# Moving two sets of quarter sums from GpSimd to VectorE in a two-layer attention kernel

## The chip, the core and the metric

The kernel runs on one core of one Trainium2 chip. The metric is the time of one execution on the device, in microseconds (us). Five engines with a queue each take part: TensorE (PE in the profile; its weight loads are PEld), VectorE (DVE), ScalarE (ACT), GpSimd (POOL) and SyncE (SP), which issues most DMAs.

## The reference, cut to what matters

Two attention blocks follow each other on `x`, 8 samples of 512 channels and 32 x 32 = 1024 positions, all in float32. The change lies in the second block, layer 1, which has one head of 512 channels:

```python
n = (x - mean) * jax.lax.rsqrt(var + EPS)          # mean and var over a whole sample
q = jnp.einsum('oc,bcs->bos', wq, nf) + bq[None, :, None]
k = jnp.einsum('oc,bcs->bos', wk, nf) + bk[None, :, None]
v = jnp.einsum('oc,bcs->bos', wv, nf) + bv[None, :, None]
attn = jnp.einsum('bci,bcj->bij', q, k) * c ** (-0.5)
attn = jax.nn.softmax(attn, axis=-1)
out = jnp.einsum('bcj,bij->bci', v, attn)
out = jnp.einsum('oc,bcs->bos', wo, out) + bo[None, :, None]
return x + out.reshape(b, c, h, w)
```

## The kernel before, in words

**Products in fewer multiplications.** Large products are made by Strassen's method in Winograd's form: both operands are cut into quarters, sums of quarters (S1 to S4 on one side, T1 to T4 on the other) are formed, and seven products of quarters replace eight. Many products use it twice: each of the seven operands is itself cut into quarters and gets its own four sums. `halve_a(name)` (L1594) makes those four second-level sums for one operand of the scores; it calls `sums_a` (L506), whose instruction is L520: four `tensor_tensor` of 128 x 256 from SBUF to SBUF, into a new buffer of the pool `t` (36 buffers of 128 x 1024, L89). The second depends on the first and the fourth on the second. A helper records them, so all have line L520; in the profile the output is `S_twice` or `A_twice` where the buffer is of pool `t`, and `spare` where it is of the weights' pool.

**Order.** PE, ACT and DVE run their instructions in the order of the program text (`manual_schedule`, L2215). `at_steps(steps, hooks)` (L765) runs a generator and, behind its n-th step, the functions listed under n: that is how side work is placed between products. `together` (L753) takes steps of two generators by turns. POOL and SP get their order from the framework's planner; POOL takes up an instruction as soon as its inputs and its buffer are free, however early that is against the other engines.

**Layer 1 of one sample**, in the order in which it runs (all samples but the last, which takes another branch and is not touched by the change):

1. A form of q is made (`make_q_twice`, L1700) in quarters `z_q` and `c_q`.
2. V is made by `make_v_twice` (L1057) through `by_two_steps` (L627): 14 steps of pairs of second-level products (steps 0 to 13, tiles `ps_s_v` and `ps_o_v`), then *V's lines*, six steps of 8 matmuls (14 to 19, tile `ps_l_v`, L793). In the pairs VectorE evicts at L644; in the lines it evicts at L665 and adds c22 onto c12 at L670 ahead of each of steps 14 and 15. Hooks here: `finish_q(1..4)` (L1780, instruction L1787, tile `s_q`) behind steps 5, 7, 9 and 11 makes the first-level sums of q, each two 128 x 512 additions on VectorE; `halve_a` of A11 behind step 3 and of S2 and S1 behind step 18, on POOL.
3. *Phase one* of the scores: `twice` (L1832) for A11*B11 and S2*T2 by turns, 14 steps of 4 matmuls (L1841, tiles `ps_l` and `ps_s`). Inside one `twice` the products go by turns into two PSUM banks, `line` (products 1, 3, 5, 7) and `single` (2, 4, 6). ScalarE copies products 1, 3, 4 and 7 to the tiles `p` (L1855), VectorE adds products 2, 5 and 6 to them (L1851). Hooks: POOL's `halve_a` of S4 and A22 (step 0), VectorE's of A12 (1) and S3 (4), and T3's sums (6).
4. *The S1 stage*: `twice` for S1*T1 alone, 7 steps. Since no other `twice` is interleaved, each product comes back to a bank two products later, and has to wait until that bank is evicted. Hooks: `onto_second(k)` (L1907) adds one 128 x 1024 tile of `p` to another on VectorE, SBUF to SBUF (L1908); `onto_third(k)` (L1910) copies its result on ScalarE; `with_p5` (L1891, instruction L1894) is another 128 x 1024 addition on VectorE.
5. *The A12/S3 phase* and *the S4/A22 phase*, 14 steps each, then the softmax's sums and the product with V.

GpSimd meanwhile runs, in this order: A11's sums, S2's, S1's, a few tiny statistics of a later sample (L350 to L356), S4's and A22's, then `sum_v` (L1966, instruction L1973, tile `s_v`): four additions of 128 x 512 of V's quarters into two buffers of pool `t`, and A12's second-level sums of V.

Of the kernel before, what the change touches and what calls it, by code (L numbers as in the profile page):

```python
# [65 lines left out]
def two_attention_blocks(  # L66
# [18 lines left out]
    nc = tc.nc  # L85
# [16 lines left out]
    def tile2(name):  # L102
        return tpool.tile([P, 2, HALF], FP, tag="t", name=name)
# [402 lines left out]
    def sums_a(q, t, engine=nc.vector, made=range(1, 5)):  # L506

        t = t if len(t.shape) == 2 else flat(t)
        n = t.shape[1] // 4
        for i in range(4):  # L510
            part = t[:, i * n : (i + 1) * n]
            if len(q["A11"].shape) == 3:
                part = part.rearrange("p (u o) -> p u o", u=2)
            q[f"S{i + 1}"] = part
        for i, x, y, op in [
            (1, "A21", "A22", ALU.add), (2, "S1", "A11", ALU.subtract),
            (3, "A11", "A21", ALU.subtract), (4, "A12", "S2", ALU.subtract),
        ]:
            if i in made:
                engine.tensor_tensor(q[f"S{i}"], q[x], q[y], op)  # L520
        return q
# [227 lines left out]
    def in_turn(*groups):  # L749
        for g in groups:  # L750
            yield from g

    def together(*groups):  # L753

        groups = list(groups)
        spares.clear()
        while groups:
            for g in list(groups):
                if next(g, g) is g:
                    groups.remove(g)  # L760
                else:
                    yield
        spares.clear()

    def at_steps(steps, hooks):  # L765

        n = -1
        for n, _ in enumerate(steps):
            for hook in hooks.get(n, []):
                hook()  # L770
        assert n >= max(hooks, default=-1)
# [209 lines left out]
    def flat(t):  # L981
        return t.rearrange("p h n -> p (h n)")
# [74 lines left out]
    def make_v_twice(w, twice_a, bs, twice_b, pairs, name):  # L1057


        parts = twice_a.all(columns_of(w))  # L1060

        def multiply(bank, n, x, y, start):
            for i, (a, v) in enumerate(PAIRS[n]):
                for u in range(2):
                    nc.tensor.matmul(  # L1065
                        bank[:, (2 * i + u) * P : (2 * i + u + 1) * P],
                        twice_b[v][y][:, u * P : (u + 1) * P], parts[a][x],
                        start=start and i == u == 0, stop=True, skip_group_check=True,
                    )

        def multiply_line(i, bank, a, v, start):
            by_positions(w.parts[0], i, bs)(bank, a, v, start)

        def at(n, r, t):
            both = flat(pairs[n][t]).rearrange("p (m o) -> p m o", m=4)
            return both[:, :, r * P : (r + 1) * P]

        return by_two_steps(multiply, multiply_line, pairs, at, None, name)
# [496 lines left out]
    def attention1(xs, norm, ready, b, at_values, norms):  # L1575
# [18 lines left out]
        def halve_a(name, t=None, engine=nc.vector):  # L1594
            q = {
                f"A{i + 1}{j + 1}": of[name][j][:, i * 2 * P : (i + 1) * 2 * P]
                for i in range(2) for j in range(2)
            }
            twice_a[name] = sums_a(q, flat(tile2(f"{name}_twice_{b}")) if t is None else t, engine)
# [131 lines left out]
        of, hooks_v, biases = {}, {}, []  # L1731
# [60 lines left out]
        if last:  # L1792
            hooks_v[17] = [lambda: halve_a("S1")]
        else:
            for n, name in [(3, "A11"), (18, "S2"), (18, "S1")]:
                hooks_v.setdefault(n, []).append(lambda name=name: halve_a(name, None, nc.gpsimd))
        at_steps(make_v_twice(w, twice_w[0], bs, twice_b, v_pairs, f"v_1_{b}"), hooks_v)


# [17 lines left out]
        def line(t):  # L1817


            bank = banks("s", f"ps_s_1_{b}_{t}")[:, 0, :]  # L1820
            c11, c12, c21 = (ps[j][t // 2][i] for i, j in [(0, 0), (0, 1), (1, 0)])
            for a, v, places in [("A11", "B11", [c11]), ("S2", "T2", [c12, c21])]:
                for k in range(2):
                    nc.tensor.matmul(  # L1824
                        bank, bs[v][:, k, t * P : (t + 1) * P], of[a][k],
                        start=a == "A11" and k == 0, stop=k == 1, skip_group_check=True,
                    )
                for to in places:
                    nc.scalar.copy(to[:, t % 2, :], bank)
                yield  # L1830
# [60 lines left out]
        def with_p5(i, j, k):  # L1891

            to, other = ps[j][k][i], ps[1][k][1] if i == 0 else ps[0][k][1]
            nc.vector.tensor_tensor(to, to, other, ALU.add)  # L1894
# [12 lines left out]
        def onto_second(k):  # L1907
            nc.vector.tensor_tensor(ps[1][k][0], ps[1][k][0], ps[0][k][0], ALU.add)  # L1908

        def onto_third(k):  # L1910
            nc.scalar.copy(ps[0][k][1], ps[1][k][0])

        if last:
            at_steps(
                together(
                    in_turn(together(line(0), line(1)), together(line(2), line(3))),
                    twice("S1", "T1", "oo", 1, 1, True, False),
                ),
                {
                    2: [lambda: halve_a("A12", spare[0])], 5: [lambda: halve_a("S3", spare[1])],  # L1920
                    8: [halve_t3], 14: [lambda: with_p5(0, 1, 0)],
                },
            )
        else:
            at_steps(
                together(
                    twice("A11", "B11", "ss", 0, 0, True, False), twice("S2", "T2", "oo", 0, 1, True, False)
                ),
                {
                    0: [lambda: halve_a("S4", None, nc.gpsimd), lambda: halve_a("A22", None, nc.gpsimd)],  # L1930
                    1: [lambda: halve_a("A12", spare[0])], 4: [lambda: halve_a("S3", spare[1])],
                    6: [halve_t3],
                },
            )
            at_steps(
                twice("S1", "T1", "so", 1, 1, True, False),
                {
                    1: [lambda: onto_second(1)], 3: [lambda: onto_second(0)], 4: [lambda: onto_third(1)],
                    6: [lambda: onto_third(0), lambda: with_p5(0, 1, 1)],
                },  # L1940
            )
# [273 lines left out]
    with tc.manual_schedule(engines={PE, ACT, DVE}):  # L2215
# [76 lines left out]
        for b in range(B):  # L2292
            xs, norm, ready, to = layer0(bs, qs, ks, vs, b, norms.get(b + 1), ending, begun)
            at_values, vs, begun = {}, [], []
            if to is not None:
                qs, ks = to["qs"], to["ks"]
                at_values = {
                    2: [lambda: vs.extend(to["v"].back())],
                    6: [lambda: put_qk(to["qk02"].back(), 0, qs, ks)],
                    10: [lambda: put_qk(to["qk13"].back(), 1, qs, ks)],  # L2300
                    14: [lambda: begun.append(first_score(qs, ks, b + 1))],
                }
            ending = attention1(xs, norm, ready, b, at_values, norms)
# [413 lines left out]
```

## Time and profile before

| what | value |
|---|---|
| time before, median of 3 runs | 2783.01 us (2782.43 to 2783.02) |
| the profiled execution's own time | 2783.47 us |
| span of its instructions | 2781.6 us |
| PE busy | 2763.5 us, 99% of the span |
| DVE busy | 2195.9 us, 79% |
| ACT busy | 1191.2 us, 43% |
| POOL busy | 685.8 us, 25% |
| granted TensorE clock | 0.999 |

The span runs from the first to the last instruction; 1.9 us of the execution's time lie around it. "Busy" is the union of the times of an engine's instructions. Matmuls overlap in the pipeline, so the time that PE loses is best read from the distance between the starts of matmuls: the 128 x 256 matmuls of V's lines and of the scores start 0.216 us apart when nothing holds them, which makes 0.86 us for a product of 4. In the timeline view each row has start, duration, engine, line, operation, out<-in and shape, and in brackets the idle time before it with the instruction that ended it; an instruction that waits inside for a resource shows as a longer duration, not as idle time.

The seven samples that the change touches follow each other 340.8 us apart, and their layer-1 stages agree within some hundredths of a us, the seventh (the one shown here, from 2386 to 2449 us) within a tenth.

### The profile page before, as it was taken

The numbers are of one execution on the slowest core, as the hardware profiler recorded it, in microseconds if no ns is written. First come the engines' busy times: TensorE is split into PE (matmuls) and PEld (weight loads), VectorE is DVE, ScalarE is ACT, GpSimd is POOL, SyncE is SP. The second block draws the span as 40 slices with busy tenths as digits, with TensorE's granted clock in tenths as the row PEclk, the third lists the DMA queues.
The fourth block names the chain that finished last, engine by engine and source line by source line (L and its number), as shares of the span: only waits on it lengthen the run. The fifth ranks groups of instructions, "written<-read, shape, count | busy, mean of one in ns | idle before, by whom it ended". The sixth has DMA issues, their size and how long they took to land. (4 is left out here: it accounts for less than half of the span.)

```text
span 2781.6 us, 42257 instructions
## 1 busy us (share of the span) xinstructions
PE 2763.5 (99%) x16486; PEld 1677.1 (60%) x16486; DVE 2195.9 (79%) x3051; ACT 1191.2 (43%) x1897; POOL 685.8 (25%) x696
## 2 busy tenths in 40 slices
PE   9999999999999999999999999999999999999999
PEld 5437774377743786447864478635686356853375
DVE  6797787877878778887788777887778877888877
ACT  3462533625346153462525524265342643226621
POOL 0001550016400263003630045300552005420121
PEclk9999999999999999999999999999999999999999
DMA  7545514264142642326432263322633236141101
GB/s 257 199 138 197 201 57 141 58 212 182 57 141 58 212 182 80 121 62 231 156 120 82 77 230 141 137 72 75 238 129 140 69 105 238 68 171 31 35 16 40
DMA packets 114528, 358.63 MB, mean 129 GB/s; under 512 B 25052, under 2 KB 25852, under 8 KB 107920
## 3 DMA queue, kind: packets, MB, share of 16 engines
q1 hardware_dynamic: 89856, 299.68, 31.5%
q10 hardware_dynamic: 24464, 56.16, 6.1%
q8 instruction: 132, 2.16, 0.3%
q14 instruction: 76, 0.62, 0.1%
HBM read 252.77 MB, written 79.21 MB: 119 GB/s over the span
## 5 line engine op out<-in xcount | busy, mean ns | idle before, releaser
L950 ACT ACTIVATE p<-s 128x1024 f32<-128x1024 f32 x505 | 516.4, 1024 | 308.4 <-PE s L1146 301.7
L952 DVE TENSOR_TENSOR acc<-acc,p 128x1024 f32<-128x1024 f32 x384 | 468.9, 1221 | 63.3 <-ACT p L950 54.3
L1146 PE MATMUL s<-qk_back,qk_back 64*64 64x512 f32 x3528 | 457.4, 590 | 0.0
L1195 PE MATMUL ps_o<-p,v_back 64*64 64x512 f32 x3528 | 455.3, 589 | 0.0
L537 POOL TENSOR_TENSOR B_twice_p<-o 128x512 f32<-128x512 f32 x14 | 20.9, 1495 | 1065.8 <-DVE o L1215 1065.8
L1195 PEld LDWEIGHTS ps_o<-p,v_back 64*64 64x64 f32 x3528 | 134.9, 133 | 243.6 <-issue 239.8
L1146 PEld LDWEIGHTS s<-qk_back,qk_back 64*64 64x64 f32 x3528 | 132.6, 133 | 245.6 <-issue 216.2
L2035 PE MATMUL ps_o<-t_p,s_v 128*128 128x512 f32 x384 | 169.6, 596 | 0.0
L1815 ACT ACTIVATE p<-p,factor 128x512 f32<-128x512 f32 (+1 forms) x112 | 85.3, 781 | 109.3 <-DVE p L1851 82.7
L537 POOL TENSOR_TENSOR B_twice<-x 128x512 f32<-128x512 f32 x23 | 38.4, 1668 | 358.6 <-DVE x L1457 177.2
L2035 PEld LDWEIGHTS ps_o<-t_p,s_v 128*128 128x128 f32 x384 | 71.8, 190 | 88.4 <-issue 88.0
L665 DVE TENSOR_TENSOR c_v<-ps_l_v,c_v 128x512 f32<-128x512 f32 x120 | 79.9, 687 | 55.1 <-PE ps_l_v L793 55.0
L1851 DVE TENSOR_TENSOR p<-ps_s,p 128x512 f32<-128x512 f32 x140 | 94.0, 685 | 30.2 <-PE ps_s L1841 28.5
L1851 DVE TENSOR_TENSOR p<-ps_l,p 128x512 f32<-128x512 f32 x150 | 101.0, 687 | 21.0 <-PE ps_l L1841 19.3
L952 DVE TENSOR_TENSOR acc<-p,p 128x1024 f32<-128x1024 f32 x57 | 69.7, 1222 | 47.8 <-ACT p L950 47.8
L1855 ACT COPY p<-ps_l 128x512 f32<-128x512 f32 x66 | 38.7, 586 | 146.9 <-PE ps_l L1841 146.9
L1044 PE MATMUL ps_l_qk<-t,w_qk 128*128 128x512 f32 x224 | 98.7, 593 | 0.1
L647 ACT COPY c_q<-ps_s_qk 128x512 f32<-128x512 f32 x56 | 32.6, 583 | 140.8 <-PE ps_s_qk L1037 140.8
L647 ACT COPY c_v<-ps_s_v 128x512 f32<-128x512 f32 x90 | 52.7, 585 | 82.3 <-PE ps_s_v L1065 80.8
L1812 POOL TENSOR_TENSOR acc<-acc,p 128x512 f32<-128x512 f32 x48 | 83.5, 1740 | 13.3 <-ACT p L1815 10.8
L373 POOL TENSOR_TENSOR rstd<-rstd,minus_half 128x4 f32<-128x4 f32 (+1 forms) x16 | 12.9, 806 | 274.2 <-DVE rstd L372 274.2
L1044 PEld LDWEIGHTS ps_l_qk<-t,w_qk 128*128 128x128 f32 x224 | 42.5, 190 | 54.0 <-issue 53.1
(709 smaller groups left out, 5965.8 us busy)
## 6 DMA issues: line engine op xcount, KB each, us to landing
x<-in_x SPq DMA_DIRECT2D x64, 512.0 KB, 8.6
qk_back<-kept_qk SPq DMA_DIRECT2D x56, 512.0 KB, 6.8
w_qk<-stored_qk SPq DMA_DIRECT2D x14, 1792.0 KB
fold<-acc SPq DMA_DIRECT2D x56, 256.0 KB, 3.0
qk_twice<-stored_qk_twice ACTq DMA_DIRECT2D x28, 512.0 KB, 4.8
kept_v<-c_v SPq DMA_DIRECT2D x28, 512.0 KB, 4.3
kept_qk<-c_q SPq DMA_DIRECT2D x28, 512.0 KB, 2.6
kept_qk<-c_k SPq DMA_DIRECT2D x28, 512.0 KB, 3.5
```

The lines of the kernel that those rows point to most:

```text
L537: engine.tensor_tensor(t[:, 0:4:2, :], part[:, :, 2 * P :], part[:, 0, :].rearrange("p (n q) -> p n q", n=2), ALU.subtract,)
L647: nc.scalar.copy(to, of(bank, to))
L665: nc.vector.tensor_tensor(c, bank, c, ALU.add)
L950: nc.scalar.activation(p, s, AF.Exp, scale=factor)
L952: nc.vector.tensor_tensor(acc, first, p, ALU.add)
L1044: nc.tensor.matmul(bank, of(i, a)[:, k, :], bs[v][:, k, :], start=start and k == 0, stop=k == 1, skip_group_check=True,)
L1146: nc.tensor.matmul(s[cols, j, :], ks[pair][k0 // HALF][rows, k0 % HALF : k0 % HALF + HD], qs[pair][g][rows, :], start=True, stop=True,)
L1195: nc.tensor.matmul(o[cols, half, :], vs[n][kt % 4 // 2][rows, h, c0 : c0 + HD], p[rows, j, :], start=kt == 0, stop=kt == NT - 1,)
L1812: engine.tensor_tensor(acc[:, i, :], acc[:, i, :], seen[i][-1], ALU.add)
L1815: nc.scalar.activation(p, p, AF.Exp, scale=norm.factor)
L1851: nc.vector.tensor_tensor(at(r, t), bank, at(r, t), ALU.add)
L2035: nc.tensor.matmul(bank, v_parts[kt // 2][a][:, kt % 2, c * P : (c + 1) * P], p_parts[kt // 2][b][:, kt % 2, cols], start=fresh and kt == ...
```

## The change

It has three parts, all in `attention1` and all for the first seven samples:

- S2's four sums go from POOL to VectorE, at the same place of the text (behind step 18 of V).
- S1's four sums go from POOL to VectorE and behind step 13, the last, of phase one.
- In the S1 stage `onto_second(0)` goes from behind the fourth product to behind the fifth's eviction, and `onto_third(1)` from behind the fifth to behind the fourth. ScalarE has no instruction between these two places, so its own order stays.

```diff
         if last:
             hooks_v[17] = [lambda: halve_a("S1")]
         else:
-            for n, name in [(3, "A11"), (18, "S2"), (18, "S1")]:
-                hooks_v.setdefault(n, []).append(lambda name=name: halve_a(name, None, nc.gpsimd))
+            hooks_v.setdefault(3, []).append(lambda: halve_a("A11", None, nc.gpsimd))
+            hooks_v[18] = [lambda: halve_a("S2")]
         at_steps(make_v_twice(w, twice_w[0], bs, twice_b, v_pairs, f"v_1_{b}"), hooks_v)
...
-                    6: [halve_t3],
+                    6: [halve_t3], 13: [lambda: halve_a("S1")],
                 },
             )
             at_steps(
                 twice("S1", "T1", "so", 1, 1, True, False),
                 {
-                    1: [lambda: onto_second(1)], 3: [lambda: onto_second(0)], 4: [lambda: onto_third(1)],
+                    1: [lambda: onto_second(1)], 3: [lambda: onto_third(1)], 4: [lambda: onto_second(0)],
                     6: [lambda: onto_third(0), lambda: with_p5(0, 1, 1)],
                 },
             )
```

## The prediction

> **What bounds the kernel now.** I read the page first, then TensorE's waits, then the timeline of each engine over one of the seven samples (the one from 2386 us), then the same stretch of the last sample.
>
> ```profile
> span 2781.6 us, 42257 instructions
> PE 2763.5 (99%) x16486; PEld 1677.1 (60%) x16486; DVE 2195.9 (79%) x3051; ACT 1191.2 (43%) x1897; POOL 685.8 (25%) x696
> ```
>
> TensorE is the bound: work taken from another engine counts only where TensorE waits for it.
>
> ```profile
> PE ps_l L1841 <- DVE p L1851: 8.0, 7, 1.2
> PE ps_l_v L793 <- DVE c_v L665: 2.6, 7, 0.4
> ```
>
> TensorE waits for VectorE at two places, seven times each: once a sample. The first is in the S1 stage (TensorE, VectorE, POOL in turn):
>
> ```profile
> 2421.22 1.05 PE L1841 MATMUL ps_s<-S_twice,t 128*128 128x256 f32 x4
> 2423.47 1.13 PE L1841 MATMUL ps_l<-s_q,T_twice 128*128 128x256 f32 x4 [1.20 <-DVE p L1851]
> ...
> 2415.01 0.69 DVE L1851 TENSOR_TENSOR p<-ps_s,p 128x512 f32<-128x512 f32 x1 [0.17 <-PE ps_s L1841]
> 2418.52 0.69 DVE L1851 TENSOR_TENSOR p<-ps_s,p 128x512 f32<-128x512 f32 x1 [2.82 <-PE ps_s L1841]
> 2419.13 3.69 DVE L1908 TENSOR_TENSOR p<-p,p 128x1024 f32<-128x1024 f32 x2
> 2422.74 0.68 DVE L1851 TENSOR_TENSOR p<-ps_l,p 128x512 f32<-128x512 f32 x1
> ...
> 2415.11 2.50 POOL L1973 TENSOR_TENSOR s_v<-c_v,c_v 128x512 f32<-128x512 f32 x2 [11.74 <-PE ps_s L1841]
> 2417.56 2.51 POOL L1973 TENSOR_TENSOR s_v<-s_v,c_v 128x512 f32<-128x512 f32 x2
> ```
>
> The seventh product (2423.47) needs the fifth's bank, whose add (2422.74) stands behind both `onto_second`. See also that VectorE idles 2.82 us ahead of 2418.52, where S1's sums are to go, and that POOL's `sum_v` starts in that hole: it waits for the same product as VectorE's add of 2415.01.
>
> The second place is V's lines: the add of 2396.71, which frees the bank, stands behind slow SBUF additions.
>
> ```profile
> 2393.82 1.84 DVE L1787 TENSOR_TENSOR s_q<-c_q,s_q 128x512 f32<-128x512 f32 x2
> 2395.57 1.21 DVE L670 TENSOR_TENSOR c_v<-c_v,c_v 128x512 f32<-128x512 f32 x1
> 2396.71 0.68 DVE L665 TENSOR_TENSOR c_v<-ps_l_v,c_v 128x512 f32<-128x512 f32 x1
> 2397.31 0.68 DVE L670 TENSOR_TENSOR c_v<-c_v,c_v 128x512 f32<-128x512 f32 x1
> ```
>
> The first L670 takes 1.21 us, the next 0.68: POOL runs S2's and S1's sums from 2389.60 to 2399.22, in turn with VectorE.
>
> **What the skill says.** "SBUF — State Buffer", section "Who interferes with whom": a VectorE instruction with two SBUF inputs contends with a GpSimd one that reads SBUF, and the first to issue has the shared port for its whole length. The trace agrees, and the last sample, where VectorE makes four 128 x 256 sums (into `spare`) beside `sum_v`, has the price:
>
> ```profile
> 2684.74 1.37 DVE L520 TENSOR_TENSOR spare<-spare,q 128x256 f32<-128x256 f32 x1
> 2686.04 1.48 DVE L520 TENSOR_TENSOR spare<-q 128x256 f32<-128x256 f32 x1
> 2687.45 1.49 DVE L520 TENSOR_TENSOR spare<-q,spare 128x256 f32<-128x256 f32 x1
> 2688.86 0.68 DVE L1851 TENSOR_TENSOR p<-ps_s,p 128x512 f32<-128x512 f32 x1
> ...
> 2683.12 2.71 POOL L1973 TENSOR_TENSOR s_v<-c_v,c_v 128x512 f32<-128x512 f32 x2 [3.18 <-issue]
> 2685.80 2.85 POOL L1973 TENSOR_TENSOR s_v<-s_v,c_v 128x512 f32<-128x512 f32 x2
> ```
>
> A sum of 0.42 us alone takes 1.48, one after each POOL addition. Adds that read PSUM (0.69 throughout) don't pay. "VectorE: DVE Perf Modes", section "The TRN2 errata", gives (N+151)/0.96 ns for a float32 addition: 424 ns at 256 columns; measured 411 to 427 without POOL.
>
> **The change part by part**, for one of seven samples. An uncontended set of four sums takes 1.46 us of VectorE (2680.25 to 2681.71 in the last sample, the same four instructions). No DMA is issued or moved; SP's queue stays. On POOL eight additions go, its other work keeps its order.
>
> *POOL loses S2's and S1's sums: -0.97.* Two losses of TensorE lie behind them. V's lines take 11.10 us (2393.35 to 2404.45) in the seven samples, but 10.36 for the same 48 matmuls in the last, where POOL is idle: 0.74. And their first matmul starts 0.37 us behind the last one before it (0.33 in the other samples; 0.11 unheld): some 0.23, since VectorE's add of `ps_o_v` (2392.62, after two `s_q` of 1.05 each) frees that bank late. Uncontended, the four last `s_q` need 4 x 0.60 instead of 2.03 + 1.75, 1.4 us less, and L670 0.5 less: more than either loss. S4's and A22's sums, next on POOL, can't start before `finish_q(4)` has ended (S4 comes first in the queue), so they meet L670 at most. Bounds: 0 (POOL fills the gap with A22 first) to -0.97; I take the whole.
>
> *S2's sums on VectorE in V's lines: +0.10.* They stand between line 0's and line 1's last adds. The first pair starts at 2402.93 and takes 1.20, the sums end at 2405.59, line 1's pair (today 2404.65) then frees its bank at 2406.87 instead of 2405.94. Phase one's fourth product starts at 2407.04 and its weight load, which takes the wait, at 2406.83: late by some 0.09. Behind them on VectorE, A12's sums and the add for product step 2 come 0.95 later; that bank is wanted at 2409.4 and is free at 2408.9. S3's and T3's sums follow without a gap until 2412.5, just when the next add falls due (2412.49): the delay is gone. Bounds 0 to +0.3.
>
> *S1's sums behind phase one, with `sum_v`: +0.93 together with the third part.* Were POOL still, they would fit the hole: 2415.62 + 1.46 = 2417.08, and product 3 wants the second sum at 2418.3. But `sum_v` waits for the buffer it writes, which the product that ends at 2415.0 releases (wait of 11.74 us; seven waits in all, 73.4 us). The change takes as many `t` buffers ahead of `sum_v` as before, so I expect it to get the same one at the same moment, 0.5 us ahead of S1's first sum. Then it goes as in the last sample: from `sum_v`'s start to the add behind the sums 2688.86 - 2683.12 = 5.74, so the add of product 2 starts at 2415.11 + 5.74 = 2420.85 instead of 2418.52. TensorE's queue stands behind it: product 4 needs that bank, 2420.85 + 0.68 + 0.05 = 2421.58 instead of 2419.27. Product 5 follows after 0.97 (as 2423.47 to 2424.44, a product behind a stall), 2422.55; product 6, held by ScalarE's copy of product 4, some 0.9 later, 2423.46.
>
> *`onto_second(0)` behind the fifth's add.* Alone it would be worth -1.31: the fifth's add would run when its product is done, and product 7 start 0.94 behind product 6, 2422.16 instead of 2423.47. After the delay above: fifth product 2422.55, its add 1.12 later (as 2417.40 to 2418.52), 2423.67, so product 7 at 2424.40; the next phase starts at 2425.37 instead of 2424.44: +0.93. The first `onto_second` ends by 2423.2 even with a POOL addition ahead, in time. The second then runs 2424.5 to 2425.7, the sixth's add and `with_p5` to 2427.4, and the first add of the A12/S3 phase at 2427.4 frees its bank by 2428.1; TensorE wants it at 2425.37 + 4 x 0.86 - 0.2 = 2428.6. Covered by 0.5; if not, 0 to +0.4.
>
> Sum: -0.97 + 0.10 + 0.93 = +0.06 a sample, times 7 = **+0.4 us**. On the profiled execution's 2783.47 that is 2783.9; that execution lies 0.46 above the median, so against 2783.01 I say **2783.4**.
>
> **The rivals.**
>
> *Few sums meet `sum_v` (faster).* For it: VectorE has a hole of 2.82 us, and POOL's start hangs on one buffer. Against: the shared wait. Without collision -0.97 + 0.10 - 1.31 = -2.18, times 7 = -15.3: 2767.7. Were `sum_v` one product (0.86) earlier, the add of product 2 comes 0.86 earlier, the stage costs +0.07, and the whole is -0.80 x 7 = -5.6: 2777.4. Chance 0.18.
>
> *POOL's turns stay in V's lines (slower).* A22's inputs are ready before `s_q`'s last sums; if POOL takes A22's four sums into the gap, each still takes its turn with an `s_q`, and V's lines keep their loss. Price +0.97 x 7 = 6.8: 2790.2. It decides if the first `A_twice<-c_q` starts before the last `s_q` has ended; against it, today it starts 0.7 us behind S4's third sum. A delay in the A12/S3 phase counts here too. Chance 0.17.
>
> **How the numbers follow.** Forecast 0.65, with its own range 2780.5 to 2787 (-0.4 to +0.5 a sample, the bounds of the small terms). What a measurement here can tell from no change is about 0.2%, 5.6 us: 2777.4 to 2788.6 is "same", 0.65; the first rival is faster, 0.18; the second slower, 0.17. The range 2776.5 to 2790 reaches the near edge of both.
>
> **What would show it.** V's lines at 10.4 us without a wait on L665; four `S_twice` on VectorE of about 1.4 us each beside `s_v`; a new wait of TensorE on L1851 at the fourth product of the S1 stage, some 2.2 us, in place of the one at the seventh; that stage 8.8 us long against 7.9. If `S_twice` takes 0.42 there, or `s_v` starts elsewhere, the prediction is wrong towards 2768; if V's lines stay at 11.1, towards 2790.

## The result, and the profile after

| | before | after | ratio, 95% interval |
|---|---|---|---|
| median of 19 runs each | 2782.86 us (2781.98 to 2783.73) | 2787.73 us (2786.16 to 2789.34) | 1.0017 [1.0010, 1.0024] |
| profiled execution | 2783.47 us | 2786.8 us | |
| its span | 2781.6 us | 2785.1 us | |

The change costs 4.9 us, 0.17%: inside the bound that the prediction set for "no change" and inside its range, but the interval excludes 1.000, and 4.3 us lie above the forecast of 2783.4. The 19 runs after lie in two groups, ten from 2786.2 to 2787.7 us and nine from 2788.3 to 2789.3; the median is the upper end of the first group, in which the profiled execution lies too. The first lines of the page after:

```profile
span 2785.1 us, 42260 instructions
PE 2761.9 (99%) x16486; PEld 1678.8 (60%) x16486; DVE 2217.3 (80%) x3107; ACT 1190.5 (43%) x1897; POOL 625.4 (22%) x640
```

56 additions (8 in each of seven samples) have gone from POOL's count to VectorE's, and 60 us of POOL's busy time with them. TensorE has the same 16486 matmuls. TensorE's waits, in total, times and longest:

```profile
PE ps_s L1841 <- DVE p L1851: 14.5, 7, 2.2
```

This one line stands where two stood before. The wait of V's lines (on L665) is gone; the wait of the S1 stage has moved from the bank `ps_l` of the seventh product to the bank `ps_s` of the fourth, and it is up to 2.2 us instead of 1.2. (The view takes the wait from the modelled end of the matmul before it. Taken from the starts of two matmuls, less the 0.216 us that one takes, TensorE idles 2.22 to 2.33 us there, before 1.30 to 1.36; these are the "idle between matmuls" below.)

One sample of the timeline after, TensorE first, then VectorE, then POOL (start, length, engine, line, operation, out<-in, shape, and in brackets the idle time before it):

```profile
1395.08 1.13 PE L1841 MATMUL ps_l<-S_twice,T_twice 128*128 128x256 f32 x4
1398.27 1.13 PE L1841 MATMUL ps_s<-S_twice,T_twice 128*128 128x256 f32 x4 [2.06 <-DVE p L1851]
1399.24 1.03 PE L1841 MATMUL ps_l<-S_twice,T_twice 128*128 128x256 f32 x4
...
1371.93 0.68 DVE L670 TENSOR_TENSOR c_v<-c_v,c_v 128x512 f32<-128x512 f32 x1
1372.75 0.69 DVE L665 TENSOR_TENSOR c_v<-ps_l_v,c_v 128x512 f32<-128x512 f32 x1
...
1392.40 0.99 DVE L520 TENSOR_TENSOR S_twice<-s_q 128x256 f32<-128x256 f32 x1
1393.42 1.38 DVE L520 TENSOR_TENSOR S_twice<-S_twice,s_q 128x256 f32<-128x256 f32 x1
1394.72 1.48 DVE L520 TENSOR_TENSOR S_twice<-s_q 128x256 f32<-128x256 f32 x1
1396.13 1.48 DVE L520 TENSOR_TENSOR S_twice<-s_q,S_twice 128x256 f32<-128x256 f32 x1
1397.54 0.68 DVE L1851 TENSOR_TENSOR p<-ps_s,p 128x512 f32<-128x512 f32 x1
...
1391.84 2.68 POOL L1973 TENSOR_TENSOR s_v<-c_v,c_v 128x512 f32<-128x512 f32 x2 [11.74 <-PE ps_s L1841]
1394.48 2.86 POOL L1973 TENSOR_TENSOR s_v<-s_v,c_v 128x512 f32<-128x512 f32 x2
```

Read it from below. `sum_v` starts with the same wait of 11.74 us as before. S1's sums on VectorE each wait for one of its additions: 0.99 us for the first, 1.38 to 1.48 for the other three, for what takes 0.42 alone. The add of product 2 therefore starts at 1397.54, 5.70 us after `sum_v`, and product 4, which needs that bank, at 1398.27. In V's lines the L670 takes 0.68 (1.21 in the sample that the prediction shows), and the L665 behind it is in time.

Up to here all is as forecast. What was not forecast is the clock, and the end of the program. First the clock. The windows view of two samples around the same wait (stretch, its length, then busy time and instructions of PE, PEld, DVE, ACT and POOL, then the granted TensorE clock):

```profile
1055.70:1058.00 2.30, 2.21 (x5) 1.85 (x6) 1.17 (x2) 0.10 (x1) 2.30 (x3) 0.52 0.00 0
1058.00:1060.00 2.00, 2.00 (x8) 1.57 (x6) 0.41 (x1) 1.43 (x2) 0.86 (x2) 0.70 0.00 0
...
1398.20:1400.00 1.80, 1.73 (x8) 1.44 (x8) 1.14 (x2) 0.56 (x2) 1.80 (x2) 1.00 0.00 0
```

In the third sample, behind the wait that ends at 1055.79, TensorE gets half its clock (0.52 and 0.70 as means of these stretches); in the fourth, behind the same wait, the whole clock. The timeline of the third sample shows what that does:

```profile
1055.79 2.07 PE L1841 MATMUL ps_s<-S_twice,T_twice 128*128 128x256 f32 x4 [2.06 <-DVE p L1851]
1057.66 1.79 PE L1841 MATMUL ps_l<-S_twice,T_twice 128*128 128x256 f32 x4
```

From product 4 to product 5 it is 1.87 us, against 0.97 in the fourth sample (1399.24 - 1398.27). By the clock records the trace holds two such stretches inside the kernel, from 1055.79 and from 2079.78, each of 3.413 us at 0.5. All 19 runs after show a mean clock of 0.998, the runs of before 0.999 or 1.000. A mean of 0.998 fits two such stretches in a run, or three; whether any had three is not on record.

**Where the time went.** Lengths by stage, from TensorE's starts, us a sample:

| | before | after, 5 samples | after, 2 samples at half clock |
|---|---|---|---|
| gap ahead of V's lines | 0.33 to 0.37 | 0.11 | 0.11 |
| V's lines | 11.10 | 10.36 | 10.36 |
| phase one | 12.09 | 12.14 | 12.14 |
| S1 stage | 7.84 to 7.90 | 8.79 to 8.85 | 10.41 and 10.45 |
| A12/S3 phase | 12.09 | 12.09 | 12.09 |
| from V's lines to those of the next sample | 340.8 (the first 341.15) | 340.8 | 342.4 and 342.5 |

Without the clock the change is worth nothing: a sample takes 340.8 us either way. The two half-clock stretches add 2 x 1.65 = 3.3 us of the span's 3.5. The rest of the two traces' difference lies outside the changed code. The first V's lines begin 1.35 us earlier after; that is not the change, for the third part alone, whose instructions are those of before up to there, begins them 1.12 us earlier than before too. And the program ends 7.6 us after its last matmul starts instead of 5.9. The last store has landed 3.4 us after that start before and 3.9 after; what follows are the semaphores by which the engines close the program (L2708). Two lines of before, then two of after, with the start of the first and of the last of the two semaphores of each queue:

```profile
L2708 ACTq EVENT_SEMAPHORE  x2: 17/17/17, 2781.0 to 2781.6; - x2
L2708 DVEq EVENT_SEMAPHORE  x2: 21/21/21, 2781.0 to 2781.6; - x2
...
L2708 ACTq EVENT_SEMAPHORE  x2: 17/17/17, 2782.8 to 2785.0; - x2
L2708 DVEq EVENT_SEMAPHORE  x2: 21/21/21, 2784.7 to 2785.0; - x2
```

Before, VectorE's first comes together with ScalarE's; after, 1.9 us later, and the next entries of the other queues follow within 0.1 us of it. The same is seen in the traces of the experiments: where VectorE's queue holds 4143 instructions, those that only wait or branch counted (the change and four of the kernels below), it comes 1.5 to 2.1 us late and the end takes 7.2 to 7.6 us; where it holds another number (before 4087, the others 4087 to 4157), it is in time and the end takes 5.6 to 5.9. Why is not shown. So the 4.9 us are, as an estimate from one trace each, 3.3 of half clock and 1.7 of this end.

### The profile page after: what moved, and what is told of

Read it like the earlier page. It is cut to its first block, busy times and chain, and to the rows that moved or that the text cites. A ratio compares the mean times of both kernels' runs of the same rounds, so it can differ in the third digit from the quotient of the medians.

```text
span 2785.1 us, 42260 instructions
## 1 busy us (share of the span) xinstructions
PE 2761.9 (99%) x16486; PEld 1678.8 (60%) x16486; DVE 2217.3 (80%) x3107; ACT 1190.5 (43%) x1897; POOL 625.4 (22%) x640
## 4 chain that ended last, share of the span: by engine, by line
PE 98%; DVE 1%; issue 0%; POOL 0%; POOLq 0%
PE ps_o L1195 16%; PE s L1146 16%; PE ps_o L2035 10%; PE ps_l L1841 6%; PE ps_l_v L793 6%; PE ps_l_qk L1044 5%; PE ps_s L1841 5%; PE ps_s_v L1065 4%; PE ps_s_qk L1037 3%; PE ps_o_v L1065 3%; PE ps_o_qk L1037 3%; PE ps_l_p L778 3%; PE ps_s_two L2165 2%; PE ps_s_p L1102 2%; PE ps_o_two L2165 1%; PE ps_o_p L1102 1%
## 5 line engine op out<-in xcount | busy, mean ns | idle before, releaser
L665 DVE TENSOR_TENSOR c_v<-ps_l_v,c_v 128x512 f32<-128x512 f32 x120 | 80.1, 688 | 56.7 <-PE ps_l_v L793 56.0
L1851 DVE TENSOR_TENSOR p<-ps_l,p 128x512 f32<-128x512 f32 x150 | 100.4, 686 | 23.1 <-PE ps_l L1841 19.3
L1851 DVE TENSOR_TENSOR p<-ps_s,p 128x512 f32<-128x512 f32 x140 | 92.5, 683 | 7.5 <-PE ps_s L1841 6.5
```

The costliest lines, as they stand in the source:

```text
L1851: nc.vector.tensor_tensor(at(r, t), bank, at(r, t), ALU.add)
```

## The experiments

Eight kernels, all timed beside the kernel before. The theory, A where an expectation uses a letter: sums pay turns to POOL's additions, the wait of product 4 is made of these turns, and it costs its length, plus 1.65 us where one clock window holds most of it. A first rival: S1's sums are harmless, and what costs is the third part, `onto_second` moved behind the fifth's add. A second rival: the half clock has nothing to do with the wait. Each expectation says in its own words what it holds against what.

### The third part alone

```diff
 # before, with only this:
-1: [lambda: onto_second(1)], 3: [lambda: onto_second(0)], 4: [lambda: onto_third(1)],
+1: [lambda: onto_second(1)], 3: [lambda: onto_third(1)], 4: [lambda: onto_second(0)],
```

> The kernel before with the third part alone: onto_second(0) behind the fifth eviction; S2's and S1's sums stay on GpSimd. Theory A (what costs is that S1's sums and sum_v take turns at the port; the reorder itself saves a wait): the S1 stage falls from 7.84 to about 6.5 us, seven times 1.31, so 2782.9 - 9.2 = 2773.7 us (ratio 0.9967), and TensorE's clock never drops. Theory B (the reorder pushes the wait to a later product or into the A12/S3 phase, and is what makes the whole change slow): 2782 to 2788 us, with a new wait behind the fifth product.

Measured 2775.07 us, ratio 0.9973 [0.9962, 0.9984]. The S1 stage takes 6.72 us (-1.12 against the -1.31 that the prediction gave it), the A12/S3 phase 12.13 (+0.04), and of the two waits of before, that on L1851 is gone and that of V's lines is left. The first rival falls: this part is a gain, and in the whole change it is eaten by the other two.

### The change without the third part

```diff
 # after, with the hooks of the S1 stage as before:
+1: [lambda: onto_second(1)], 3: [lambda: onto_second(0)], 4: [lambda: onto_third(1)],
-1: [lambda: onto_second(1)], 3: [lambda: onto_third(1)], 4: [lambda: onto_second(0)],
```

> The change without its third part: S2's and S1's sums on VectorE as in the change, both onto_second in their old places. Theory A: the wait at the fourth product stays, and the fifth product's add then stands behind both onto_second, product 7 about 0.5 us later than in the change: 3.5 us more than the change, about 2791 us. Theory B (the reorder is what costs): faster than the change, 2780 us or less.

Measured 2788.27 us, ratio 1.0019 [1.0013, 1.0026]: below what was expected. The stage is 9.32 us, 0.53 longer than after, as it should be, which is 3.7 us; but its trace has no half-clock stretch inside the kernel, which gives 3.3 back, and the spans of the two are equal. That trace is of the shortest of 20 runs. Ten of them take 2786.9 to 2787.8 us, ten 2788.8 to 2789.2, 1.7 us apart in the median, which would be one half-clock stretch in each of the longer ones; no trace of those was kept, so this is not shown. Its wait of product 4 is as long as in the change (14.5 us in seven). A wait of 2.2 us alone doesn't halve the clock, then; where it falls must matter. That is read off below.

### S2's sums alone on VectorE

```diff
 # before, with S2's sums on VectorE, S1's still on POOL:
-for n, name in [(3, "A11"), (18, "S2"), (18, "S1")]:
-    hooks_v.setdefault(n, []).append(lambda name=name: halve_a(name, None, nc.gpsimd))
+hooks_v.setdefault(3, []).append(lambda: halve_a("A11", None, nc.gpsimd))
+hooks_v[18] = [lambda: halve_a("S2"), lambda: halve_a("S1", None, nc.gpsimd)]
```

> The kernel before with S2's sums alone on VectorE in V's lines; S1's stay on GpSimd, onto_second stays. Theory A: S1's four sums on GpSimd now meet only the third set of s_q sums, V's lines fall from 11.10 to 10.36 us, the gap ahead of them stays some 0.2 us long, phase one's fourth product comes 0.05 late, the S1 stage stays 7.84: 0.7 us less a sample, 2782.9 - 4.9 = 2778.0 us (ratio 0.9982). Theory C (VectorE's sums in V's lines cost more than GpSimd's turns gave back): 2783 us or more.

A miss: 2784.76 us, ratio 1.0007 [0.9999, 1.0015]. V's lines take 10.36 us and the gap is 0.11, so the whole gain came. But in six of the seven samples phase one is 13.62 us. VectorE and POOL in one of them, then TensorE's waits:

```profile
357.63 0.95 DVE L520 TENSOR_TENSOR S_twice<-s_q 128x256 f32<-128x256 f32 x1
358.62 0.83 DVE L520 TENSOR_TENSOR S_twice<-S_twice,s_q 128x256 f32<-128x256 f32 x1
...
356.90 0.73 POOL L520 TENSOR_TENSOR S_twice<-s_q,S_twice 128x256 f32<-128x256 f32 x1
357.58 0.73 POOL L520 TENSOR_TENSOR A_twice<-A_twice,c_q 128x256 f32<-128x256 f32 x1
```

```profile
PE ps_s L1841 <- DVE c_v L665: 7.8, 6, 1.3
```

POOL's sums of S1 come first in its queue, so its sums of S4 and A22 slip to where VectorE now makes S2's: 0.95 and 0.83 us instead of 0.42, the last adds of V's lines (L665) late behind them, and a new wait of 1.3 us. In the change S1's sums are gone from POOL too, S4's and A22's end before S2's begin (VectorE's four S2 sums take 0.41 to 0.42 there), and the term is +0.05.

### S1's sums four steps earlier

```diff
 # after, with one number changed:
-6: [halve_t3], 13: [lambda: halve_a("S1")],
+6: [halve_t3], 9: [lambda: halve_a("S1")],
```

> The whole change, but S1's sums behind step 9 of phase one instead of step 13, so that they are done at about the moment at which sum_v starts. Theory A (turns with sum_v): the four sums take some 0.42 us each, V's lines stay at 10.36 us, the S1 stage takes about 6.5 us, no drop of the clock: 0.97 - 0.05 + 1.31 = 2.23 us less a sample than before, 2782.9 - 15.6 = 2767.3 us (ratio 0.9944). Theory C (VectorE's added eight sums a sample cost wherever they stand, by late evictions): 2783 us or more. Theory D (the clock drops come from something else than the idle of TensorE in the S1 stage): two or more drops of 1.65 us remain.

Measured 2772.20 us, ratio 0.9961 [0.9947, 0.9974]: faster than both. The same four sums take 0.42 us each, the last of them just as `sum_v` starts; the S1 stage is 6.60 us, V's lines 10.36, phase one 12.14, and no half-clock stretch is left inside the kernel. So it is the meeting with `sum_v` that costs, not the sums. It stays 5 us above what was expected. 3.3 of them are the A12/S3 phase, which takes 12.56 us (+0.47): with the stage 2.2 us shorter, both `onto_second` and `with_p5` fall beside POOL. The other 1.6 are the late end of the program, 7.6 us as in the change.

```profile
1392.81 1.72 DVE L1908 TENSOR_TENSOR p<-p,p 128x1024 f32<-128x1024 f32 x1
...
1395.23 1.77 DVE L1894 TENSOR_TENSOR p<-p,p 128x1024 f32<-128x1024 f32 x1
...
1391.04 1.71 POOL L520 TENSOR_TENSOR A_v_twice<-c_v,c_v 128x256 f32<-128x256 f32 x1
...
1393.40 1.71 POOL L520 TENSOR_TENSOR A_v_twice<-A_v_twice,c_v 128x256 f32<-128x256 f32 x1
```

Alone each of the two VectorE additions takes 1.2 us. Note that the loss is mutual: POOL's sum of 0.73 takes 1.71 when VectorE has the port.

### Two of S1's sums later: less idle at once

```diff
 # after, with halve_a able to make some of the four sums:
-6: [halve_t3], 13: [lambda: halve_a("S1")],
+6: [halve_t3], 13: [lambda: halve_a("S1", made=[1, 2])],
...
-1: [lambda: onto_second(1)], 3: [lambda: onto_third(1)], 4: [lambda: onto_second(0)],
+1: [lambda: halve_a("S1", made=[3, 4]), lambda: onto_second(1)], 3: [lambda: onto_third(1)], 4: [lambda: onto_second(0)],
```

> The changed kernel, with S1's four sums split: the first two stay behind phase one's last step, the other two are issued behind the add of product 2 in the S1 stage, ahead of the first onto_second. The sums are the same; all of them still meet sum_v, but TensorE's wait is cut in two. The theory (turns with POOL, and a TensorE clock that is halved for 3.41 us when its window holds too much idle time): the wait ahead of product 4 shrinks by the two turns, from 2.2 us to at most 1.4, the other turns come back as a smaller wait later, no sample shows a halved clock, V's lines stay at 10.36 us, the S1 stage takes about 8.0 us, and the kernel about 2778 us (2774 to 2783). The rival, that the halved clock of two samples has nothing to do with the idle time (say, something that happens once in so many us): two or three samples still show it, and 3 to 5 us more are taken.

Measured 2779.63 us, ratio 0.9989 [0.9982, 0.9995]. The largest of TensorE's waits:

```profile
PE ps_l L1843 <- DVE p L1853: 7.5, 7, 1.1
```

The same sums pay the same turns, but TensorE idles in two pieces (1.2 us between two matmuls and a smaller one), and no sample has a half clock. The stage is 8.28 us in six samples and 7.71 in the last, a little more than expected.

### One of S1's sums made three times: more idle

```diff
 # after, with the fourth sum written twice more:
-13: [lambda: halve_a("S1")],
+13: [lambda: halve_a("S1")] + [lambda: halve_a("S1", made=[4])] * 2,
```

> The changed kernel, with S1's fourth quarter sum made twice more behind phase one (the same values written again): two more VectorE sums that each take a turn with a POOL addition, so the wait ahead of product 4 grows from 2.2 to some 4.0 us. If the idle time of one clock window decides, the clock is halved in nearly every sample (6 or 7 of 7, against 2), each for 1.65 us or more: 2784.3 (the change without drops) + 7 x 1.8 + 7 x 1.65 = 2808 us (2803 to 2812). If the drops of two samples are not from the idle time: the wait grows alike, but drops stay at about two: 2784.3 + 12.6 + 3.3 = 2800.

Measured 2809.19 us, ratio 1.0096 [1.0080, 1.0111], beside an expected 2808. TensorE's wait, and two stretches behind it in one sample:

```profile
PE ps_s L1843 <- DVE p L1853: 26.6, 7, 3.9
```

```profile
1754.60:1757.00 2.40, 2.34 (x6) 1.89 (x7) 1.13 (x2) 0.23 (x1) 1.66 (x1) 0.50 0.00 0
1757.00:1760.00 3.00, 3.00 (x9) 2.44 (x8) 1.42 (x2) 1.30 (x2) 0.00 (x0) 0.54 0.00 0
```

All seven samples run at half clock behind the wait, one for 3.413 us, six for 6.827, twice that. With 1.7 us of wait more, the stage grows by 3.1 to 4.1 us.

### Product 2 made twice: the same wait, less idle

```diff
 # after, in `twice`:
 multiply(single, "A12", "B21", True)
+if tags == "so":                         # the S1 stage alone
+    multiply(single, "A12", "B21", True)  # again, over the first
 add(single, 0, 0)
```

> The changed kernel, with product 2 of the S1 stage multiplied twice (the second time over the first, the same values), so that TensorE has 0.86 us of work more ahead of the wait for product 4's bank. That wait ends when VectorE is done with S1's sums and product 2's add, so the stage should stay 8.8 us long while the idle time shrinks from 2.2 to 1.4 us. If idle time in one clock window causes the halved clock: no drop in any sample, and the kernel runs like the change without its drops, 2786.8 - 2 x 1.65 = 2783.5 us (2782.5 to 2784.5), with runs closer together than the change's (2786.2 to 2789.3). If the halving comes from elsewhere: drops stay, 2786 to 2789. If product 4 does not stand behind the add of product 2 but behind TensorE's own work: the stage is 0.86 longer, 2783.5 + 6.0 = 2789.5.

This is the sharpest test, since TensorE does more work. Measured 2784.49 us, ratio 1.0006 [0.9997, 1.0014], 3.2 us less than the change, with 28 matmuls more.

```profile
PE ps_s L1841 <- DVE p L1851: 9.4, 7, 1.4
```

The S1 stage is 8.80 us as in the change, since product 4 still stands behind the same add; the time between two matmuls is 1.50 us instead of 2.23, and no sample has a half clock. A sample takes 340.8 us, as before; of the 1.9 us that this kernel still lies above before, the late end of the program (7.6 us) makes 1.6. The second rival falls: the clock follows TensorE's idle time.

### A12's sums of V later as well

```diff
 # the kernel with S1's sums at step 9, and:
-if not last:
-    halve_v("A12", nc.gpsimd)
...
-{4: [lambda: c22(1)], 5: [] if last else [lambda: halve_p("B22", nc.gpsimd)]},
+{4: [lambda: c22(1)], 5: [] if last else [lambda: halve_p("B22", nc.gpsimd), lambda: halve_v("A12", nc.gpsimd)]},
```

> The changed kernel, with S1's sums behind step 9 of phase one (as in the run with step 9) and POOL's sums of A12 for the values (A_v_twice) put behind its sums of B22, so that they don't meet onto_second and with_p5. The turns theory: the second onto_second takes 1.2 us instead of 1.72 and with_p5 1.2 instead of 1.77, VectorE is 1.1 us earlier at the A12/S3 phase, whose fourth product no longer waits: 12.1 us instead of 12.56, 7 x 0.45 = 3 us less than with step 9 alone, 2769 (2767 to 2771). A rival: A12's sums then delay POOL's additions onto acc and with them the sums of rows, so that the values wait and the 3 us or more are given back: 2772 to 2777.

Measured 2769.69 us, ratio 0.9953 [0.9940, 0.9967], the fastest of all. The second `onto_second` and `with_p5` in it:

```profile
374.81 1.22 DVE L1908 TENSOR_TENSOR p<-p,p 128x1024 f32<-128x1024 f32 x1
...
376.74 1.23 DVE L1894 TENSOR_TENSOR p<-p,p 128x1024 f32<-128x1024 f32 x1
```

The A12/S3 phase is back at 12.09 us. But the expectation's rival came in part as well: the values, L2033, show one wait of up to 0.3 us a sample that wasn't there. So a sample takes 338.97 us against 339.13, and from the first V's lines to the last matmul the two traces differ by 0.8 us. The time fell by 2.5 us because the program also ends early again, 5.6 us after the last matmul starts instead of 7.6: that 2769 was met is in good part luck.

## Why the prediction was nearly right, point by point

- **POOL loses the sums, -0.97: right.** V's lines -0.74, the gap -0.22 to -0.26, in every sample, and in the run with S2's sums alone as well. The bound of 0, that POOL fills the gap with A22's sums, didn't come. One line was misread: the turns of S2's and S1's eight sums end at 2397.4, and what runs on to 2399.22 are the first sums of S4; the loss is the same.
- **S2's sums in V's lines, +0.10: right, +0.05 measured.** It is that small only because S1's sums leave POOL too: with S1's sums still there it was +1.5.
- **S1's sums with `sum_v`, and the third part, +0.93 together: right, +0.95.** The add of product 2 came 5.70 us behind `sum_v` (5.74 forecast), the wait is 2.2 us at the fourth product, the stage 8.8 us. Each half was tried: the third part alone gives -1.12, the sums without it +1.48 (9.32 against 7.84), and moved out of `sum_v`'s way they cost the stage nothing. "SBUF — State Buffer", section "Who interferes with whom", of the Trainium skill says that the shared port is locked by one instruction while the other engine waits; that the two then go by turns, one instruction each, is what the trace adds, with the lengths.
- **The A12/S3 phase, "Covered by 0.5": right for the change** (12.09 both times). But the cover was only that deep: with the stage 2.2 us shorter it was gone and cost 0.47, at the top of the 0 to +0.4 stated "if not".
- **Sum +0.06 a sample: right** (340.8 us against 340.8). **What failed is the step from that sum to the time**, "+0.06 a sample, times 7 = +0.4 us". It takes each wait at its length, as if TensorE ran behind a wait of 2.2 us as behind one of 1.3. Two of seven samples lose another 1.65 us behind it: +3.3 us that no term of the sum held. Nor did one hold the end of the program, +1.7 us. The two waits of before, together 1.5 us a sample, lay apart; the change put 2.2 us into one place.

What the idle time must be for that can be read from the runs. "TensorE: Matmul & The Clock Gate", section "What's actually happening", of the Trainium skill says that the clock is decided in windows of 3413 ns that run freely and don't begin anew with the kernel. The trace agrees: a half-clock stretch lasts 3.413 us or twice that, and the two of the change begin 1024.0 us apart, 300 times 3.4133. Every trace also ends at half clock, behind the last matmul; in the change that stretch begins 703.15 us behind the second one, 206 times 3.4133. So its start gives the edges where a kernel has no stretch inside. With the windows laid on these edges, the share of the window that the idle time leaves to TensorE can be worked out for each sample:

| kernel | idle between matmuls | busy share of the window that holds most of it | half clock |
|---|---|---|---|
| before | 1.30 to 1.36 | 0.60 to 0.74 | none of 7 |
| product 2 twice | 1.50 to 1.55 | 0.56 to 0.73 | none of 7 |
| after | 2.22 to 2.33 | 0.35 and 0.38 | 2 of 2 |
| after | | 0.50 to 0.66 | none of 5 |
| without the third part | 2.22 to 2.33 | 0.58 to 0.60 | none of 7 |
| fourth sum three times | 3.95 to 4.06 | 0.26 to 0.35 | 7 of 7 |

So at whole clock a window at most 0.38 busy is followed by a half-clock one, and one at least 0.50 busy isn't (one of 0.49 in the last kernel wasn't either); the bound lies between 0.38 and 0.49. A wait of 2.2 us falls into one window or is split over two, by where the sample stands in the grid. In the change a sample takes 340.8 us, 99.85 windows, so the wait drifts through the grid and meets the bad place twice in seven; without the third part a sample takes 341.33 us, 100.00 windows, and in the traced run the wait was split over two windows of some 0.75 and 0.60 in every sample. That explains why the slower code there was not slower, and it is luck, not design: a run that begins elsewhere in the grid can meet the bad place. A stretch then moves the next wait by 1.65 us, half a window, so an estimate from these figures is one stretch or two in such a run and not seven, and the two groups of its 20 runs fit that. The section "HAM oscillation — how this bites in real kernels" gives as the rule no idle gap over some 3.4 us; here the measurement decides, and 2.2 us was enough.

What stays open: why the program ends 1.7 us later where VectorE's queue holds 4143 instructions, and whether the longer of the 19 runs after held a third half-clock stretch, so that the split of the 4.9 us is that of the traced run.

## What to carry to other kernels

Moving work off a contended engine helps only if it lands where the other holder of the port is still: the same four sums made the S1 stage 2.2 us longer at one hook than four steps earlier (1.7 us a sample, since 0.47 came back behind it), so look for when the other engine's queue starts, not only for a hole in this one. Price TensorE's waits not by their sum but by their place: one of 2.2 us cost 3.9 where it met the clock window badly, the same turns split in two cost no clock, and repeating a product ahead of the wait can be cheaper than idling. And when a stage is made shorter, work out again what was covered behind it. Before a small gain is put down to a stage, look at what lies outside all stages: 1.6 to 2.0 us of four of the differences here came behind the last matmul.

## What the runs showed of the hardware that was not expected

- An idle time of TensorE of 2.2 us, well under one clock window, halved its clock for 3.413 us when it fell mostly into one window (busy share 0.38 or less). Where a wait of 4 us reached on into the halved window and left it 0.47 to 0.58 busy, the clock stayed halved for one more (six samples), though 0.50 had not halved a whole clock.
- Work that is thrown away can shorten the time: 28 matmuls more than in the change, 3.2 us less.
- In the port's turns both sides pay: VectorE's 0.42 us becomes 1.4 to 1.5 beside additions of 128 x 512 and 0.83 to 0.95 beside those of 128 x 256; POOL's 0.73 becomes 1.71 beside VectorE's 128 x 1024.
- At the end of the program, behind the last store, VectorE's closing semaphore came 1.5 to 2.1 us behind ScalarE's in the five kernels whose VectorE queue holds 4143 instructions, and together with it in the other five.
